# A two-layer attention kernel: other PSUM tiles and an earlier split for the first attention, and another layout for its group norm

## The chip, the cores and the metric

The kernel runs on one core of a Trainium2 chip. The metric is the device time of one launch in microseconds, and the number that counts is the median over repeated runs. Beside the times there is one execution that the hardware profiler recorded; durations of single instructions come from it.

## The reference

The input is 8 images of 32 x 32 positions with 384 channels, all in float32. Two layers are computed, each adding to the residual:

```python
# layer 0
g = group_norm(x)                        # 32 groups of 12 neighbouring channels, over all positions
q, k, v = split(g @ qkv_w + qkv_b)       # 6 heads of 64
s = (q * 64**-0.5) @ k.T + rel_h + rel_w # rel_h[q, kh] = q . table_h[h - kh + 31], rel_w likewise
x = x + softmax(s) @ v @ proj_w + proj_b
# layer 1
t = tokens(x)
a = layer_norm(t)
t = t + softmax(causal((a @ Wq) @ (a @ Wk).T * 384**-0.5)) @ (a @ Wv)   # one head of 384
t = t + ffn(layer_norm(t))   # two linear layers with weights binarised to signs, each output
                             # quantised by the absolute maximum of a group of images; gelu between
```

The quantisation groups are formed over images and only five images get an FFN output; the other three get zero from it.

## The kernel before, in words

The program is written with a tile framework. The author writes the work image by image, and the framework puts the instructions of each engine in an order of its own, with semaphores between engines; each engine then works its queue strictly in that order. Tiles come from pools with a fixed number of buffers: a tile that is asked for when all buffers are taken waits for the oldest to be released. `image` and `page` are SBUF pools with 11 buffers each, `small` has 3. In PSUM there are two score tiles of two banks each (`s_tile`, 128 x 1024) and four tiles of one bank (`o_tile`, 128 x 512).

The stages of one image in layer 0 are these.

- **Group norm** (`group_norm_T`, L299 to L325). The image is loaded channel-major by `load_T` (L293) in three tiles of 128 x 1024. Partition p holds the three neighbouring channels 3p, 3p+1 and 3p+2 (`"(p k) t -> p k t"`), so that a group of 12 is four neighbouring partitions. VectorE takes the statistics of the three channels of a partition together (L306, L307). TensorE sums over the four partitions with the constant matrix `over_group`, once for the mean (L310) and once for the variance (L317). Between these stand small VectorE operations (L312, L314, L315, L318), the square root on ScalarE (L319) and the reciprocal (L320); then the three tiles are normalised (L322). For image b+1 all this runs inside layer 1's attention of image b.
- **Projections** (`queries_keys`, L416). For m = 0 to 5 a 128-column block of the weights gives two heads of q (m = 0 to 2) or k (m = 3 to 5), for the whole image in one two-bank score tile (`project_T`, L361). For each half ScalarE writes the high part (L426, rounded to the matmul's input format) and VectorE the rest (L429). k is also copied with its halves swapped (`ks`, DMAs at L435).
- **Position tables** (`positions`, L443). The products of q with both tables are made in one-bank tiles (L452), copied to a page by ScalarE (L456) and VectorE (L457), and written to DRAM (`far`, L461). DMAs with a shifted stride read the needed diagonals back (`near`, L468).
- **Splits** (`split`, L473). Each 32-row piece of `near` is rounded by ScalarE (L479), the rest is made by VectorE (L480), and both go into `r`, which enters the scores as a third matmul against the constant `unit`. `split(0)` and `split(1)` stand before and after the v projections; `split(2)` is deferred into the attention for every image but the first:

```python
            split(0, near[0])
            for j in range(NJ):
                values(j)
            split(1, near[1])
            later = [lambda: split(2, near[2])]
            if b == 0 or not pools.fast:
                later.pop()()
```

- **v** (`values`, L484): eight projections (L371), copied alternately by ScalarE and VectorE (L485).
- **Attention** (`attend0_fast`): for three pairs of heads p and eight chunks c of keys, scores (L527), exp on ScalarE into a page (L531), running sums on VectorE (L540), and the product with v (L545). The residual with the projection's bias is added on GpSimd (L510).

Layer 1 has its scores at L735, its exp at L743 and its product with v at L749. Its two projection matrices are folded into one by `multiply_out` (wq @ wk.T), which for image 0 loads both matrices and multiplies them just ahead of the first attention. The FFN's last step for image b (`unfinished`) is run inside the projections of image b+1, after m = 3. A second, general path is entered only when the fast path found an overflow; it isn't run here.

Of the kernel before, what the change touches and what calls it, by code (L numbers as in the profile page):

```python
# [27 lines left out]
NP_GN = P // GROUPS_GN  # L28
# [46 lines left out]
def conv_attn_hybrid(  # L75
# [42 lines left out]
    def load_weights(pools):  # L118
# [9 lines left out]
        src = qkv_w.rearrange("(p k) o -> p k o", k=NC)  # L128
# [29 lines left out]
    over_group = const.tile([P, P], F32, name="over_group")  # L158
    nc.gpsimd.memset(over_group, 1.0 / NP_GN)
    for low in (True, False):  # L160

        nc.gpsimd.affine_select(
            out=over_group, in_=over_group, compare_op=ALU.is_ge, fill=0.0, base=0 if low else NP_GN - 1,
            pattern=[[-NP_GN if low else NP_GN, GROUPS_GN], [0, NP_GN]], channel_multiplier=1 if low else -1,
        )
# [104 lines left out]
    def multiply_out(pools):  # L270
# [3 lines left out]
        nc.sync.dma_start(out=wkT_sb, in_=wkT.rearrange("(k p) c -> p k c", p=P))  # L274
        for m in range(NC):
            ps = pools.o_tile(f"wqk_{m}")
            for k in range(NC):
                nc.tensor.matmul(ps[:, :C], wqT_sb[:, k, ts(m, P)], wkT_sb[:, k, :], start=(k == 0), stop=(k == NC - 1))
            nc.vector.tensor_scalar_mul(wqk[:, m, :], ps[:, :C], C**-0.5)

    def stages(pools):
# [9 lines left out]
        def load_T(b):  # L291

            xT = pools.image(f"gnT_{b}")  # L293
            src = img_T[b].rearrange("(p k) t -> p k t", k=NC)
# [4 lines left out]
        def group_norm_T(b, xT=None):  # L299
# [3 lines left out]
            mv = pools.small.tile([P, 2], F32, tag="gmv", name=f"gmv_{b}")  # L303
# [3 lines left out]
            nc.vector.bn_aggr(mv, st.rearrange("p k a s -> p (k a s)"))  # L307

            ps = pools.o_tile(f"gmean_{b}")
            nc.tensor.matmul(ps[:, 0:1], over_group, mv[:, 0:1], start=True, stop=True)  # L310
            cs = pools.small.tile([P, 2], F32, tag="gcs", name=f"gcs_{b}")
            nc.vector.tensor_copy(cs[:, 0:1], ps[:, 0:1])  # L312
            d = pools.small.tile([P, 2], F32, tag="gd", name=f"gd_{b}")
            nc.vector.tensor_tensor(d[:, 0:1], mv[:, 0:1], cs[:, 0:1], ALU.subtract)  # L314
            nc.vector.scalar_tensor_tensor(d[:, 1:2], d[:, 0:1], d[:, 0:1], mv[:, 1:2], ALU.mult, ALU.add)  # L315
            ps = pools.o_tile(f"gvar_{b}")
            nc.tensor.matmul(ps[:, 0:1], over_group, d[:, 1:2], start=True, stop=True)  # L317
            nc.vector.tensor_scalar_add(d[:, 0:1], ps[:, 0:1], 1e-5)  # L318
            nc.scalar.activation(d[:, 0:1], d[:, 0:1], AF.Sqrt)  # L319
            nc.vector.reciprocal(cs[:, 1:2], d[:, 0:1])  # L320
            for k in range(NC):
                nc.vector.tensor_scalar(  # L322
                    xT[:, k, :], xT[:, k, :], cs[:, 0:1], cs[:, 1:2], ALU.subtract, ALU.mult
# [83 lines left out]
        def layer0(b, xT):  # L407
# [8 lines left out]
            def queries_keys(m):  # L416
                p = m % NPAIR
                bias = bqk[:, m : m + 1]
                ps = project_T(wqkv_sb, ts(m, P), xT, f"qk_{b}_{m}")
                dst = [(q if m < NPAIR else k)[par][:, p, :] for par in range(2)]  # L420

                for half in range(2):
                    t = ts(half, T // 2)
                    for par in range(2):
                        hi = rows[par]
                        nc.scalar.activation(dst[par][hi, t], ps[hi, t], AF.Identity, bias=bias[hi])  # L426
                    for par in range(2):
                        hi, lo = rows[par], rows[1 - par]
                        nc.vector.scalar_tensor_tensor(  # L429
                            dst[par][lo, t], ps[hi, t], bias[hi], dst[par][hi, t].bitcast(F32), ALU.add, ALU.subtract  # L430
# [12 lines left out]
            def positions(p):  # L443

                fars = []
                for par in range(2):
                    page = pools.page(f"far_{b}_{p}_{par}")
                    by_col = page.rearrange("i (w h) -> i w h", h=H)
                    for half in range(2):
                        ps = pools.o_tile(f"rel_{b}_{p}_{par}_{half}")  # L450
                        for i in range(2):
# [523 lines left out]
```

## Time and profile before

| what | value |
|---|---|
| median of 8 runs | 2580.23 us (2577.38 to 2581.87) |
| the profiled execution | 2577.29 us, its span 2575.6 us |
| TensorE matmul busy | 2498.8 us, 97% of the span |
| VectorE busy | 1614.4 us, 63% |
| ScalarE busy | 1156.6 us, 45% |
| GpSimd busy | 113.8 us, 4% |
| DMA | 144.70 MB, mean 56 GB/s |
| mean granted TensorE clock | 0.998 of full speed |

The span runs from the first to the last recorded instruction; 1.7 us of the launch lie around it. Busy times of the engines overlap. In the profile PE is TensorE's matmuls, PEld its weight loads, DVE is VectorE, ACT is ScalarE, POOL is GpSimd and SP the queue that issues most DMAs. A float32 matmul of the program is two matmul rows in the profile, one in the rounded format is one. "Idle before, releaser" says how long an engine had nothing to do before an instruction, and what it waited for.

### The profile page before, as it was taken

To read this page: it belongs to the slowest core of one execution; us is meant where nothing else is said; L and a number is where in the kernel's file an instruction comes from. 1 tells how busy PE (TensorE), PEld (TensorE's weight loads), DVE (VectorE), ACT (ScalarE), POOL (GpSimd) and SP (SyncE) were. 2 spreads that over 40 slices of the span, in tenths; PEclk is the share of its full clock that TensorE was granted. 3 is DMA by queue.
4 is the path that set the end of the run, shared out by engine and by line. 5 is a ranking of instruction groups with operands and counts; after the bars stand their busy time and mean duration, and the time that the engine had idled before them with its cause. 6 is when DMAs were issued, how large, how long until landed. Compare 5 with 4: busy or idle time off the path is not lost. (4 is left out here: it accounts for less than half of the span.)

```text
span 2575.6 us, 24797 instructions
## 1 busy us (share of the span) xinstructions
PE 2498.8 (97%) x9378; PEld 1495.0 (58%) x9378; DVE 1614.4 (63%) x2375; ACT 1156.6 (45%) x1513; POOL 113.8 (4%) x103
## 2 busy tenths in 40 slices
PE   7999999999999999999999999999999999999998
PEld 3555685555765556755557555576555555555554
DVE  5895468763587644786546876447764486538652
ACT  4641377421666314764127643156641264127420
POOL 0000002000011000110000100001100010001000
PEclk9999999999999999999999999999999999999999
DMA  6431106011041101150110601003200240015000
GB/s 169 148 147 62 37 1 172 1 62 37 1 123 49 49 13 37 41 131 1 61 37 1 172 1 62 17 21 94 79 25 1 70 103 1 25 42 130 1 1 26
DMA packets 148992, 144.70 MB, mean 56 GB/s; under 512 B 107264, under 2 KB 129664, under 8 KB 147328
## 3 DMA queue, kind: packets, MB, share of 16 engines
q1 hardware_dynamic: 142928, 119.36, 16.5%
q0 software_dynamic: 2880, 23.59, 2.6%
q8 instruction: 76, 1.25, 0.2%
q10 hardware_dynamic: 3056, 0.08, 0.1%
q14 instruction: 52, 0.43, 0.1%
HBM read 75.38 MB, written 42.47 MB: 46 GB/s over the span
## 5 line engine op out<-in xcount | busy, mean ns | idle before, releaser
L531 ACT ACTIVATE f_pr<-f_s 128x1024 f32<-128x1024 f32 x384 | 392.7, 1027 | 401.9 <-PE f_s L527 372.4
L540 DVE TENSOR_TENSOR f_sum<-f_sum,f_pr 128x1024 f32<-128x1024 f32 x288 | 349.0, 1244 | 145.9 <-ACT f_pr L531 144.0
L545 PE MATMUL f_av<-f_pr,f_v 128*64 128x512 f32 x1536 | 359.5, 599 | 0.0
L527 PE MATMUL f_s<-f_q,f_k 128*128 128x512 f32 x768 | 258.2, 417 | 22.5 <-ACT f_pr L531 15.6
L361 PE MATMUL f_qk<-f_gnT,wqkv_sb 128*128 128x512 f32 x576 | 261.7, 599 | 7.3 <-DVE f_k L429 3.3
L527 PE MATMUL f_s<-f_q,f_ks 128*128 128x512 f32 x768 | 244.1, 399 | 0.0
L527 PE MATMUL f_s<-f_r,unit 128*128 128x512 f32 x768 | 241.7, 396 | 0.0
L545 PEld LDWEIGHTS f_av<-f_pr,f_v 128*64 128x64 f32 x1536 | 103.0, 136 | 202.4 <-issue 194.6
L480 DVE TENSOR_TENSOR f_r<-f_near,f_r 32x1024 fp32r<-32x1024 f32 x96 | 193.2, 2012 | 28.7 <-ACT f_r L479 25.9
L527 PEld LDWEIGHTS f_s<-f_q,f_k 128*128 128x128 f32 x768 | 125.0, 189 | 139.2 <-issue 51.9
L735 PE MATMUL f_s<-f_q,f_lnT 128*128 128x512 f32 (+3 forms) x576 | 197.2, 488 | 0.0
L749 PE MATMUL f_av<-f_v,f_pr 128*128 128x385 f32 x576 | 194.5, 486 | 0.0
L361 PEld LDWEIGHTS f_qk<-f_gnT,wqkv_sb 128*128 128x128 f32 x576 | 108.0, 191 | 123.5 <-issue 110.0
L527 PEld LDWEIGHTS f_s<-f_q,f_ks 128*128 128x128 f32 x768 | 145.2, 189 | 35.8
L527 PEld LDWEIGHTS f_s<-f_r,unit 128*128 128x128 f32 x768 | 144.9, 189 | 34.4
L749 PEld LDWEIGHTS f_av<-f_v,f_pr 128*128 128x128 f32 x576 | 108.6, 190 | 78.6 <-issue 11.5
L479 ACT CAST f_r<-f_near 32x1024 fp32r<-32x1024 f32 x96 | 145.9, 1520 | 2.4
L735 PEld LDWEIGHTS f_s<-f_q,f_lnT 128*128 128x128 f32 x576 | 101.4, 190 | 73.9 <-issue 50.2
L371 PE MATMUL f_v<-wqkv_sb,f_gnT 128*128 128x384 f32 x384 | 129.4, 490 | 10.5 <-ACT f_v L485 8.3
L850 DVE TENSOR_REDUCE am<-f_h 128x1 f32<-128x1024 f32 (+2 forms) x80 | 71.6, 946 | 96.6 <-ACT f_h L843 96.6
L843 ACT ACTIVATE f_h<-f_y,b_sb 128x256 f32<-128x256 f32 x240 | 100.8, 472 | 67.0 <-PE f_y L839 67.0
L743 ACT ACTIVATE f_pr<-f_s 128x1024 f32<-128x1024 f32 (+3 forms) x64 | 41.7, 651 | 194.4 <-DVE f_s L740 194.4
(153 smaller groups left out, 3325.4 us busy)
## 6 DMA issues: line engine op xcount, KB each, us to landing
f_far<-f_far SPq DMA_DIRECT2D x48, 512.0 KB, 3.0
f_ks<-f_k SPq DMA_DIRECT2D x96, 256.0 KB, 5.1
f_gnT<-in_xT SPq DMA_DIRECT2D x24, 512.0 KB, 4.6
f_near<-f_far SPq DMA_DIRECT2D x96, 128.0 KB, 3.8
f_x<-in_x SPq DMA_DIRECT2D x32, 384.0 KB, 6.7
out_y<-f_x SPq DMA_DIRECT2D x32, 384.0 KB, 4.0
f_w1a<-w1s POOLq DMA_DIRECT2D x5, 1536.0 KB, 7.2
f_w2a<-w2s POOLq DMA_DIRECT2D x5, 1536.0 KB, 6.7
```

The costliest lines, as they stand in the source:

```text
L361: nc.tensor.matmul(ps[:, half, :], w[:, k, cols], xT[:, k, ts(half, 512)], start=(k == 0), stop=(k == NC - 1),)
L371: nc.tensor.matmul(ps[:, :C], xT[:, k, ts(j, P)], w[:, k, cols], start=(k == 0), stop=(k == NC - 1))
L479: nc.scalar.copy(dst[ts(hi, 32)], src)
L480: nc.vector.tensor_tensor(dst[ts(lo, 32)], src, dst[ts(hi, 32)].bitcast(F32), ALU.subtract)
L527: nc.tensor.matmul(sc[:, half, :], keys[:, ts(c, P)], queries[:, ts(half, 512)], start=(i == 0), stop=(i == 2))
L531: nc.scalar.activation(pr, sc.rearrange("p a n -> p (a n)"), AF.Exp)
L540: nc.vector.tensor_tensor(sums[par], prev, prs[par], ALU.add)
L545: nc.tensor.matmul(avs[half][ts(par, HD), :], v[:, c, ts(h, HD)], prs[par][:, ts(half, 512)], start=(c == 0), stop=(c == NJ - 1),)
L735: nc.tensor.matmul(sc[:, half, lo:], xT[:, c // 4, k, ts(c % 4, P)], q[:, half, k, lo:], start=(k == 0), stop=(k == NC - 1),)
L749: nc.tensor.matmul(av[:, : C + 1], prs[c][:, ts(j - c, P)], v[:, c, :], start=(c == 0), stop=(c == j))
L843: nc.scalar.activation(pairs[i][:, m, :, :], ps[:, ts(i % 2, 256)].rearrange("p (j q) -> p j q", j=2), AF.Identity, bias=b1_sb[:, m : m + 1],)
L850: nc.vector.tensor_reduce(am[:, i, n - 1 : n], pairs[i][:, cuts[n - 1] : cuts[n], :, :], AX.XYZ, ALU.max, apply_absolute_value=True)
```

## The change

Six things are changed together.

1. Group norm: the channels are laid out in the usual way, channel 128 k + p on partition p (`"(k p) t -> p k t"`, for the weights too). A group of 12 lies across partitions of one tile or of two. Statistics are taken per channel, and each step over groups is three small matmuls: to 32 groups with `to_group` (L326), and back to the channels with `of_group` (L334), for the mean and again for mean and scale. So there are four steps instead of two.
2. k (and q of image 0) is projected into a one-bank tile per half (L457). q of the other images stays in score tiles.
3. The table products of p = 1 and 2 (and of all p for image 0) go into score tiles, with one copy of 64 x 1024 on each engine (L499, L500).
4. The splits of p = 1 and 2 are made for both heads at once (`split_both`, L521 and L522) into the pages that held the tables, and eight DMAs per pair bring the rows to `r` (L526). All are written ahead of the attention; nothing is deferred.
5. After `unfinished`, a one-element exp with scale 0 is run on ScalarE.
6. wq.T and wk.T are loaded at the start (`load_qk`, L282), and `multiply_out` stands among the first image's projections.

```diff
         def load_T(b):
             xT = pools.image(f"gnT_{b}")
-            src = img_T[b].rearrange("(p k) t -> p k t", k=NC)
+            src = img_T[b].rearrange("(k p) t -> p k t", p=P)
...
-            nc.vector.bn_aggr(mv, st.rearrange("p k a s -> p (k a s)"))
-            ps = pools.o_tile(f"gmean_{b}")
-            nc.tensor.matmul(ps[:, 0:1], over_group, mv[:, 0:1], start=True, stop=True)
-            cs = pools.small.tile([P, 2], F32, tag="gcs", name=f"gcs_{b}")
-            nc.vector.tensor_copy(cs[:, 0:1], ps[:, 0:1])
-            d = pools.small.tile([P, 2], F32, tag="gd", name=f"gd_{b}")
-            nc.vector.tensor_tensor(d[:, 0:1], mv[:, 0:1], cs[:, 0:1], ALU.subtract)
-            nc.vector.scalar_tensor_tensor(d[:, 1:2], d[:, 0:1], d[:, 0:1], mv[:, 1:2], ALU.mult, ALU.add)
-            ps = pools.o_tile(f"gvar_{b}")
-            nc.tensor.matmul(ps[:, 0:1], over_group, d[:, 1:2], start=True, stop=True)
-            nc.vector.tensor_scalar_add(d[:, 0:1], ps[:, 0:1], 1e-5)
-            nc.scalar.activation(d[:, 0:1], d[:, 0:1], AF.Sqrt)
-            nc.vector.reciprocal(cs[:, 1:2], d[:, 0:1])
+                nc.vector.bn_aggr(mv[:, k, :], st[:, k, :, :].rearrange("p a s -> p (a s)"))
+            def over_groups(src, name):
+                ps = pools.o_tile(name)
+                for k in range(NC):
+                    nc.tensor.matmul(
+                        ps[:GROUPS_GN, 0:1], to_group[:, k, :], src(k), start=(k == 0), stop=(k == NC - 1)
+                    )
+                return ps[:GROUPS_GN, 0:1]
+            def to_channels(src, n, name):
+                ps = pools.o_tile(name)
+                for k in range(NC):
+                    nc.tensor.matmul(ps[:, k * n : (k + 1) * n], of_group[:, ts(k, P)], src, start=True, stop=True)
+                return ps[:, : NC * n].rearrange("p (k n) -> p k n", k=NC)
+            gm = pools.small.tile([GROUPS_GN, 2], F32, tag="gm", name=f"gm_{b}")
+            nc.vector.tensor_copy(gm[:, 0:1], over_groups(lambda k: mv[:, k, 0:1], "gmean"))
+            mc = to_channels(gm[:, 0:1], 1, "cmean")
+            d = pools.small.tile([P, NC, 1], F32, tag="gd", name=f"gd_{b}")
+            nc.vector.tensor_tensor(d, mv[:, :, 0:1], mc, ALU.subtract)
+            nc.vector.tensor_tensor(d, d, d, ALU.mult)
+            nc.vector.tensor_tensor(d, d, mv[:, :, 1:2], ALU.add)
+            var = pools.small.tile([GROUPS_GN, 1], F32, tag="gvar", name=f"gvar_{b}")
+            nc.vector.tensor_scalar_add(var, over_groups(lambda k: d[:, k, :], "gvar"), 1e-5)
+            nc.scalar.activation(var, var, AF.Sqrt)
+            nc.vector.reciprocal(gm[:, 1:2], var)
+            cs = pools.small.tile([P, NC, 2], F32, tag="gcs", name=f"gcs_{b}")
+            nc.vector.tensor_copy(cs, to_channels(gm, 2, "cstat"))
...
             def queries_keys(m):
-                ps = project_T(wqkv_sb, ts(m, P), xT, f"qk_{b}_{m}")
+                both = project_T(wqkv_sb, ts(m, P), xT, f"qk_{b}_{m}") if b and m < NPAIR else None
                 for half in range(2):
                     t = ts(half, T // 2)
+                    if both is None:
+                        ps = pools.o_tile(f"qk_{b}_{m}_{half}")
+                        for i in range(NC):
+                            nc.tensor.matmul(
+                                ps, wqkv_sb[:, i, ts(m, P)], xT[:, i, t], start=(i == 0), stop=(i == NC - 1)
+                            )
+                    else:
+                        ps = both[:, t]
...
             def positions(p):
-                    for half in range(2):
-                        ps = pools.o_tile(f"rel_{b}_{p}_{par}_{half}")
...
+                    n = 1 + (p > 0 or b == 0)
+                    for part in range(2 // n):
+                        ps = pools.s_tile(f"rel_{b}_{p}_{par}") if n == 2 else pools.o_tile(f"rel_{b}_{p}_{par}_{part}")[:, None, :]
...
+                        nc.scalar.copy(page[:HD, ts(part, n * 512)], ps[:HD])
                         nc.vector.tensor_copy(
+                            by_col[HD:, :, ts(part, n * H // 2)], ps[HD:].rearrange("i (h w) -> i w h", w=W)
                         )
...
+            def split_both(p, near, pages):
+                for d in range(2):
+                    hi, lo, src = (t[ts(d, HD)].rearrange("k (h w) -> k h w", h=H) for t in (*pages, near))
+                    if d:
+                        src = near[ts(d, HD)].rearrange("k (w h) -> k h w", h=H)
+                    nc.scalar.copy(hi, src)
+                    nc.vector.tensor_tensor(lo, src, hi.bitcast(F32), ALU.subtract)
+                for i in range(2):
+                    for d in range(2):
+                        for par in range(2):
+                            nc.sync.dma_start(
+                                out=r[par][ts(2 * i + d, 32), p, :].bitcast(F32),
+                                in_=pages[i][ts(2 * d + par, 32)].bitcast(F32),
+                            )
...
+                if m == NPAIR + 1 and sides_qk:
+                    multiply_out(pools, *sides_qk.pop())
                 if m == NPAIR and unfinished:
                     unfinished.pop()()
+                    early = pools.small.tile([P, 1], F32, tag="early", name=f"early0_{b}")
+                    nc.scalar.activation(early, k[1][:, 0, T - 1 :].bitcast(F32), AF.Exp, scale=0.0)
+                if m == NPAIR + 1:
+                    split(0, near[0][0])
-            split(0, near[0])
             for j in range(NJ):
                 values(j)
-            split(1, near[1])
-            later = [lambda: split(2, near[2])]
-            if b == 0 or not pools.fast:
-                later.pop()()
+            split_both(1, *near[1])
+            split_both(2, *near[2])
             if pools.fast and b == 0:
                 join_biases(pools)
-                multiply_out(pools)
...
         def run(pools):
             gn = load_T(0)
             if pools.fast:
                 load_weights(pools)
+                sides_qk.append(load_qk(pools))
```

## The prediction, made before the changed kernel was run

> **What bounds the kernel now.** I read the page first, then TensorE's waits, then busy time over the eight stretches that the change rebuilds, then the timelines of ACT, PE and DVE where a wait ends.
>
> The page (engine, busy us, share, instructions; then the granted clock by slice):
>
> ```profile
> span 2575.6 us, 24797 instructions
> ...
> PE 2498.8 (97%) x9378; PEld 1495.0 (58%) x9378; DVE 1614.4 (63%) x2375; ACT 1156.6 (45%) x1513; POOL 113.8 (4%) x103
> ...
> L479 ACT CAST f_r<-f_near 32x1024 fp32r<-32x1024 f32 x96 | 145.9, 1520 | 2.4
> ```
>
> TensorE is the bound: 2575.6 - 2498.8 = 76.8 us idle. A change can win only from those holes, or from TensorE's own work. Its waits (who waited for whom: us, times, longest):
>
> ```profile
> PE f_s L527 <- ACT f_pr L531: 15.6, 15, 1.9
> PE f_gmean L310 <- DVE gmv L307: 11.3, 1, 11.3
> PE f_v L371 <- ACT f_v L485: 8.3, 8, 1.1
> ...
> PE f_s L527 <- DVE f_k L429: 4.1, 5, 0.8
> ...
> PE f_qk L361 <- DVE f_k L429: 3.3, 5, 1.0
> ...
> PE f_s L527 <- ACT f_far L456: 2.8, 3, 0.9
> PE f_v L371 <- DVE f_far L457: 2.2, 5, 0.5
> ```
>
> Seven kinds, nearly all where an image goes from projections into attention. That stage by image 0, 1, 2, 5, 6, 7 (length; PE, PEld, DVE, ACT, POOL busy; clock):
>
> ```profile
> 50.00:92.00 42.00, 36.38 (x120) 21.75 (x118) 33.29 (x32) 36.66 (x37) 0.00 (x0) 1.00 0.74 187
> 388.00:446.00 58.00, 52.87 (x165) 28.23 (x163) 49.17 (x59) 44.04 (x51) 12.66 (x10) 1.00 0.74 190
> 733.00:791.00 58.00, 52.95 (x165) 28.28 (x164) 49.05 (x59) 44.06 (x51) 12.76 (x10) 1.00 0.73 190
> ...
> 1769.00:1827.00 58.00, 53.48 (x165) 29.71 (x165) 47.65 (x58) 43.05 (x51) 12.86 (x10) 0.97 0.71 190
> 2040.00:2098.00 58.00, 55.27 (x169) 29.41 (x168) 45.61 (x46) 44.30 (x53) 6.77 (x1) 1.00 0.66 163
> 2309.00:2367.00 58.00, 55.20 (x170) 29.38 (x169) 45.51 (x46) 44.48 (x53) 7.56 (x1) 1.00 0.66 163
> ```
>
> PE idle is length less busy: 5.62, 5.13, 5.05, 4.52, 2.73, 2.80; images 3 and 4 have 5.32 and 5.11, together 36.3 us. The worst hole, on ACT in image 5:
>
> ```profile
> 1813.25 0.48 ACT L485 COPY f_v<-f_v 128x384 f32<-128x384 f32 x1
> 1813.75 1.28 ACT L531 ACT_TABLE_LOAD   x1
> 1815.04 1.94 ACT L531 ACTIVATE f_pr<-f_s 128x1024 f32<-128x1024 f32 x2
> ```
>
> TensorE, out of score tiles, resumes at 1816.12 after 1.87 us; the table load is most of it. The group norm as it now runs inside layer 1's attention:
>
> ```profile
> 1982.13 0.28 PE L310 MATMUL f_gmean<-gmv,over_group 128*128 128x1 f32 x2
> 1982.27 1.96 PE L735 MATMUL f_s<-f_q,f_lnT 128*128 128x512 f32 x4
> 1984.07 0.28 PE L317 MATMUL f_gvar<-gd,over_group 128*128 128x1 f32 x2
> 1984.21 1.96 PE L735 MATMUL f_s<-f_q,f_lnT 128*128 128x512 f32 x4
> ```
>
> Score rows start right behind it: no stop.
>
> **What one stop costs.** Idle is not all. Paired score rows on an undisturbed path start 0.46 us apart (780.37 to 780.83), the first pair after the stop at 779.80 takes 0.57: 0.11 more. And a row shown as 0.39 long has its successor 0.23 later, so 0.16 of each hole is drawn as busy. A stop costs its idle plus 0.27.
>
> **The parts.**
>
> *k in one-bank tiles, table products in two-bank tiles, splits ahead.* ACT's second half of k no longer waits behind VectorE's 0.75 us L429 on the same tile; the far copies are one 64x1024 on each engine instead of two of 64x512; the splits of p 1 and 2 become 2 + 2 instructions per pair instead of 4 + 4. By L479's 1.52 us mean, four ACT casts fewer per image are 6.1 us, and about as much on VectorE. Both run beside TensorE (ACT 44 of 58 us busy, VectorE 49), so this counts only through the holes. Image 2, walked in the changed program's order with before's durations: 0.521 and 0.827 (k), 0.441 (far) and 0.336 vanish. The v wait of 1.03 shrinks to 0.5: ACT still runs casts ahead of the v copy. New: about 0.9 at a two-bank product that waits for qk_2's score tile, and 0.2 at v_3.
>
> *exp's table early* (images 1 to 5; in 6 and 7 the sqrt and exp loads are elsewhere, and their hole here is 0.4). The 1.28 us load and one tiny activation move to ACT's slack beside the k projections (14 of 58 us), and the 1.9 us hole goes; next late is the v copy. If ACT were late there, 1.28 would come back at k. The Trainium skill, "ScalarE: Activation LUTs", section "What ACT_TABLE_LOAD costs", puts each switch at about 2.66 us, 1.28 of load and 1.38 of drain. The row shows no drain: copy ends 1813.73, load 1813.75 to 1815.03, exp 1815.04. By the page the five holes would shrink by 5 x 1.38 = 6.9 us more than I count.
>
> *What comes in.* The split rows are now written into the far pages and carried to r by 16 more 128 KB DMAs per image on SP. Near's DMAs of that size land in 3.8 us; p=1's rows are wanted some 40 us later. They stand behind the ks DMAs on SP, but ahead of f_x, whose add on POOL (L510, 7.2 us, up to 8.0) starts later; f_x has slack. The pages stay taken longer, and VectorE's last split subtraction stands ahead of the first sums (L540, 1.24 us each), which free pages for exp. I expect a wait of 1.0 us in image 1 to 5 (0 if the sums keep up, 2 if not; middle taken). The order also divides one more av pair per image there: a lone pair holds the queue 1.01 us (2089.32 to 2090.33) instead of 0.43; I take 0.4, as part replaces one that exists now.
>
> Images 1 to 5: idle 25.13 / 5 = 5.03, plus 6 stops x 0.27 = 6.65 now. After: 0.9 + 0.2 + 0.5 + 3 x 0.27 = 2.41, page wait 1.27, pair 0.4: 4.08. Gain 2.6 each, 13.0 in all (bounds: nothing to 5 each).
> Images 6, 7: 2.77 + 4 x 0.27 + 0.6 (a divided pair, gone) = 4.45 now; after 0.5 + 0.4 + 2 x 0.27 = 1.44. Gain 3.0 each, 6.0.
>
> *Clock.* In 1816.3 to 1819.7 the granted clock was 0.51, right behind the 1.87 us hole, and likewise behind the 1.82 us hole at 1470.5: 3.4 us at half pace, 1.7 lost, twice. Without those holes, 3.4 gained (0 if another hole triggers it). The Trainium skill, "TensorE: Matmul & The Clock Gate", section "What's actually happening", lets the clock fall only after about 3.4 us of idleness; holes of 1.8 would be harmless and this term would be 0. The rows have the drop, so I keep 3.4.
>
> *Image 0.* Idle 5.62 + 5 x 0.27 = 6.97. The wq @ wk.T matmuls (18 rows, about 0.32 us each by 384-column v rows) fill among the projections, but the exp load stays; I take half, 3.5 (0 to 6). Against it the longer start: gmean to gvar took 11.29 to 12.54 with two cold loads of 0.25 per step; four steps of six, less the sqrt load's present wait, make 3.3 (2 to 4.5). The wqT and wkT loads (1.18 MB) now stand on SP among the start's loads: at the 169 GB/s of the page's first slice 7 us of transfer, over before the first table product's DMA (first far copy at 30.3); no cost taken, up to 2 in the bounds. Together +0.2.
>
> *Group norm, images 1 to 7.* 24 tiny rows instead of 4, in four steps, with TensorE's order putting one score matmul pair (0.86) between steps. A load of 128 columns costs 0.11 (two gmean rows push the scores by 0.22). Twelve such: 1.3. Twelve of 32 columns, not in the trace, cost between 0.03 and 0.11 each by width and by that row: middle 0.8. Less today's 0.45: 1.65. Hops: matmul to VectorE 0.29, 0.15 to 0.22 per operation, three operations at the longest: about 0.9 against 0.94 cover. A v copy (0.56) may stand ahead on VectorE, as at 1982.34; 0.25 for that. 1.9 each (1.2 to 3.5): 13.3 lost.
>
> **Sum.** 13.0 + 6.0 + 3.4 + 0.2 - 13.3 = 9.3 us. The profiled execution took 2577.29 (span 2575.6 plus 1.7 around it), 2.94 below the median 2580.23. 2577.3 - 9.3 = 2568.0, and on the median 2571. About 0.2% (5.2 us) is what a measurement here can tell from no change.
>
> **Rivals.**
> 1. *Pages (slower).* The sums fall under POOL's 7.2 us add (VectorE's L480 took 8.52 at worst where 1.2 is usual), pages run out and exp of p=0 stops, so score tiles do. For: less room on 11 pages, far ones held. Against: VectorE has 16% slack and PE's waits on exp are short. Beyond 2.3 us per image (9.3 / 8 more than I count, plus my 1.0) the gain is gone; at 4 extra x 8 = 32, about 2603. Chance 0.14.
> 2. *Hops stop TensorE (slower).* If the three further hops are not covered, each costs up to what 11.29 to 12.54 shows, 1.25: 7 x 3 x 1.25 = 26 more, 2597; at half, 2584. For: cover is equal to the hop by 0.04. Chance 0.14.
> 3. *The holes only move.* ACT still does casts ahead of v and VectorE is no shorter: images 1 to 5 gain 1.5 instead of 2.6, images 6 and 7 1.5 instead of 3.0: 8.5 less, 2579.5. For: L480's 1.9 us median on VectorE is as long in the new form, and v still waits for ACT. Against: the table load alone is 1.28 of each 1.9 us hole. Chance 0.16.
> 4. *All holes go.* 5 x 5 + 2 x 4 + 3.4 + 1 - 10 = 27: 2553. For: ACT and VectorE have 14 and 9 us free per stage. Against: the walk finds four new or left waits. Chance 0.14.
> My forecast: 0.42.
>
> Range 2554 to 2590: it leaves out rival 1's upper part and the little below rival 4. Faster (below 2575) 0.60: rival 4, 0.39 of the forecast's 0.42, 0.07 of rival 3. Same 0.14: 0.03 of the forecast, 0.07 of rival 3, 0.04 of rival 2. Slower (above 2585.4) 0.26: rival 1, 0.10 of rival 2, 0.02 of rival 3.
>
> **What would show it.** Right: PE idle in the stage of images 1 to 5 near 3 us, no hole of 1.8 us on exp, no clock of 0.5 mid-run, tiny matmul steps 0.5 to 0.9 us apart from the scores with little idle, first projection of image 0 about 3 us later. Wrong: waits of PE on f_pr in p=0 above 2 us, behind L540's successor; idle behind the group means' matmuls; r's DMAs landing late.

## The result

The changed kernel takes 2586.25 us (median of 11 runs, 2578.49 to 2588.14) against 2579.76 for the kernel before (31 runs): the ratio is 1.0023, with a 95% interval of 1.0015 to 1.003. It is 6 us slower, where 9 us less had been forecast. Its profiled execution took 2580.74 us, 5.5 less than the median; the run with GpSimd's add moved (below) shows what that difference may be.

The page of the changed kernel, the same two lines as before:

```profile
span 2579.0 us, 25377 instructions
...
PE 2521.3 (98%) x9538; PEld 1509.4 (59%) x9538; DVE 1554.5 (60%) x2341; ACT 1104.2 (43%) x1452; POOL 106.0 (4%) x106
```

TensorE's idle time fell from 76.8 to 57.7 us, as the change meant it to, but its busy time rose by 22.5: partly the group norm's rows, partly rows that ran at half clock. Its waits:

```profile
PE f_s L587 <- ACT f_pr L591: 9.0, 17, 1.1
...
PE f_den L647 <- DVE f_sum L600: 5.0, 1, 5.0
PE f_den L635 <- ACT f_oT L624: 4.5, 1, 4.5
...
PE f_v L401 <- ACT f_v L543: 0.5, 3, 0.2
```

The waits on k and on the table copies are gone, the one on v fell from 8.3 to 0.5. Two single waits of 5.0 and 4.5 us are new. The next view shows the stage between projections and attention in images 2, 5 and 6, then the two stretches at half clock (start and end; length; PE, PEld, DVE, ACT, POOL busy; clock):

```profile
744.90:802.90 58.00, 57.68 (x191) 32.71 (x190) 46.28 (x56) 40.28 (x47) 5.46 (x9) 1.00 0.83 207
1781.00:1839.00 58.00, 57.65 (x192) 32.08 (x192) 46.02 (x55) 40.52 (x46) 5.46 (x9) 1.00 0.89 221
2048.00:2106.00 58.00, 57.80 (x187) 31.54 (x185) 39.48 (x42) 39.23 (x46) 0.00 (x0) 1.00 0.73 170
148.80:155.60 6.80, 5.02 (x15) 3.96 (x16) 6.01 (x20) 3.95 (x5) 0.48 (x1) 0.50 0.01 3
206.80:213.70 6.90, 5.42 (x9) 1.77 (x10) 3.85 (x5) 0.00 (x0) 5.24 (x1) 0.51 0.37 151
```

Idle in the stage is 0.2 to 0.4 us, where 4.5 to 5.1 (images 2 and 5) and 2.7 (image 6) stood before. So the stage did better than forecast, and the time went elsewhere. Distances between the starts of matching score rows in the two traces say where. When image 0's layer 1 begins, the changed kernel is 10.1 us behind; each of seven group norms adds 2.41 us, 16.9 in all; each first attention of images 1 to 7 wins back 2.8 to 4.0, 24 in all. 10.1 + 16.9 - 24 = 3, the difference of the spans (3.4).

Image 0 is the surprise. The two new stops, on ACT, on TensorE and on VectorE:

```profile
148.95 1.07 ACT L624 COPY f_oT<-f_av 128x512 f32<-128x512 f32 x2 [11.27 <-DVE sums_w L240]
```

```profile
149.59 0.43 PE L635 MATMUL f_den<-few,fold 128*64 128x32 f32 x4 [4.53 <-ACT f_oT L624]
151.00 1.22 PE L587 MATMUL f_s<-f_q,f_k 128*128 128x512 f32 x2 [0.99 <-ACT f_pr L591]
```

```profile
134.69 7.36 DVE L240 TENSOR_REDUCE sums_w<-f_w 128x1 f32<-128x614 f32 x15
141.97 3.48 DVE L600 TENSOR_TENSOR f_sum<-f_sum,f_pr 128x1024 f32<-128x1024 f32 x3
145.37 3.55 DVE L240 TENSOR_REDUCE sums_w<-f_w 128x1 f32<-128x608 f32 x5
```

In image 0 VectorE also takes the sums and signs of the FFN weights. The attention output f_oT needs a buffer of the pool in which those raw weights lie, and gets it when the reductions L240 have read them. They run at 134.7 to 148.9, 37 us later than before, when they began at 97.6 and ended at 116.8. Two of their rows in the kernel before:

```profile
97.60 1.48 DVE L228 TENSOR_REDUCE sums_w<-f_w 128x1 f32<-128x614 f32 x2
...
113.20 3.55 DVE L228 TENSOR_REDUCE sums_w<-f_w 128x1 f32<-128x608 f32 x5
```

In the changed kernel ACT stands at the copy for 11.3 us, with the exps behind it, and TensorE stops; the signs come late as well, and the sums of p = 2 behind them.

### The profile page after: what moved, and what is told of

It is laid out like the page before. It is cut to its first block, busy times and chain, and to the rows that moved or that the text cites. A ratio compares the mean times of both kernels' runs of the same rounds, so it can differ in the third digit from the quotient of the medians.

```text
span 2579.0 us, 25377 instructions
## 1 busy us (share of the span) xinstructions
PE 2521.3 (98%) x9538; PEld 1509.4 (59%) x9538; DVE 1554.5 (60%) x2341; ACT 1104.2 (43%) x1452; POOL 106.0 (4%) x106
## 3 DMA queue, kind: packets, MB, share of 16 engines
q8 instruction: 78, 1.28, 0.2%
## 4 chain that ended last, share of the span: by engine, by line
PE 88%; ACT 5%; DVE 4%; issue 1%; DMA 1%; ACTq 0%; POOL 0%; POOLq 0%; DVEq 0%
PE f_s L587 20%; PE f_av L605 12%; PE f_v L401 8%; PE f_s L793 7%; PE f_av L807 7%; PE f_y L897 6%; PE f_qk L457 5%; PE f_q L755 5%; PE f_y L936 4%; PE f_qk L391 4%; PE f_pj L401 2%; PE f_rel L494 2%; PE f_pj L690 2%; ACT f_r L537 1%; PE f_pt L303 1%
## 5 line engine op out<-in xcount | busy, mean ns | idle before, releaser
L600 DVE TENSOR_TENSOR f_sum<-f_sum,f_pr 128x1024 f32<-128x1024 f32 x288 | 379.5, 1351 | 150.2 <-ACT f_pr L591 149.0
L807 PEld LDWEIGHTS f_av<-f_v,f_pr 128*128 128x128 f32 x576 | 108.6, 190 | 78.6 <-issue 11.5
L457 PE MATMUL f_qk<-f_gnT,wqkv_sb 128*128 128x512 f32 x324 | 147.3, 602 | 1.2 <-DVE f_gnT L352 1.2
L755 PE MATMUL f_q<-f_lnT,wqk 128*128 128x512 f32 x288 | 127.5, 592 | 0.0
L401 PE MATMUL f_v<-wv_sb,f_lnT 128*128 128x384 f32 x384 | 126.5, 486 | 0.0
```

Source lines behind the costliest of these rows:

```text
L401: nc.tensor.matmul(ps[:, :C], xT[:, k, ts(j, P)], w[:, k, cols], start=(k == 0), stop=(k == NC - 1))
L457: nc.tensor.matmul(ps, wqkv_sb[:, i, ts(m, P)], xT[:, i, t], start=(i == 0), stop=(i == NC - 1))
L600: nc.vector.tensor_tensor(sums[par], prev, prs[par], ALU.add)
L755: nc.tensor.matmul(ps, wqk[:, k, ts(m, P)], xT[:, half, k, :], start=(k == 0), stop=(k == NC - 1))
L807: nc.tensor.matmul(av[:, : C + 1], prs[c][:, ts(j - c, P)], v[:, c, :], start=(c == 0), stop=(c == j))
```

## The experiments

All times are medians, and every kernel was timed beside the kernel before, which took 2580.85 to 2583.44 us in these comparisons. The changed kernel itself was timed only in the first comparison, at 2586.25. "Less" and "more" are against that, unless another kernel is named; such differences are good to some 3 us, and smaller ones say nothing.

**The loads on another queue.** My first theory was SP's queue: the raw weights' first load is issued at 95.8 us (74.1 before), behind the 16 split DMAs.

```diff
-                    nc.sync.dma_start(out=w, in_=...)
+                    (nc.gpsimd if name == "w" else nc.sync).dma_start(out=w, in_=...)
```

> The changed kernel, with one edit: the loads of the raw FFN weights that feed the sums over groups are issued by GpSimd instead of SP, so that they no longer stand behind the 16 new split DMAs of image 0. Queue theory: these loads start at 74 us or earlier (95.8 in the changed kernel), VectorE's reductions over them run before 120 us again (134.7 to 149 now), the attention output of image 0 gets its buffer in time, and TensorE's stops of 4.5 + 1.0 us near 150 us and 5.1 us near 208 us go, with the half clock behind both: 13 to 17 us less, 2570 to 2573. Rival, pages: the sums of image 0 are late because the split holds VectorE and the pages; then the queue of the weight loads matters little, and the time stays within 4 us of 2586.

2577.45 (0.9981, 0.9972 to 0.999): 9 less, not 13 to 17. The reductions run at 79 to 101 now, but a stop of 6.2 us on exp stands at 102.6, since the sums that free pages wait behind reductions, and one of 2.3 at 214.7. The stops moved; the queue was not all of it.

**The old split in image 0 alone.**

```diff
-                        at = 2 * d + par if p else 2 * par + d
+                        at = 2 * d + par if p and b else 2 * par + d
...
-            split_both(1, *near[1])
-            split_both(2, *near[2])
+            for p in (1, 2):
+                split_both(p, *near[p]) if b else split(p, near[p][0])
```

> The changed kernel, but image 0 splits p = 1 and 2 the old way, in 32-row pieces straight into r, so it issues no split DMAs; images 1 to 7 are as in the changed kernel. Queue theory: as in the run with the other queue, 10 to 17 us less (2569 to 2576), with the weight loads on SP right behind the ks DMAs near 75 us. Theory that the early products of wq and wk and the buffer of their weights, and not the queue, make the attention output of image 0 wait: the stops remain, and the time is within 4 us of 2586.

2577.16 (0.9981, 0.9973 to 0.999), again 9 less. The first loads are issued at 70.9 to 81.5, earlier than in the kernel before up to the second one, yet the reductions start at 110.5, not 97.6: they stand behind ten sums in VectorE's queue. Stops of 3.2 and 3.8 us are left. So early loads do not make early reductions.

**The old group norm,** code as in the front part.

> The changed kernel with the group norm of the kernel before (three neighbouring channels on a partition, two steps of one matmul), everything else as changed. From the distances of the score rows in the two traces the new group norm costs 2.4 us on TensorE for each of seven images and 1.2 us at the start: 18 us less, 2568. Rival: part of that time covers waits that would come back elsewhere (exp or sums), and only half is won, about 2577. The stops of image 0 stay in either case.

2567.74 (0.9942, 0.9927 to 0.9957): 18.5 less. Six executions lie between 2562 and 2570, so the median alone is good to some 4 us; seven times 2.41 and 1.2 at the start, by distances of score rows in the traces, make 18.1. The stops of image 0 stay (4.5, 1.0 and 5.1 us). The norm's cost is its own.

**Both edits.**

> Both of the last two edits at once: the old group norm, and the old split in image 0. If the two costs are independent, their gains add: 18 + 10 to 17, so 2551 to 2558, some 25 us faster than the kernel before. If the stops of image 0 hang on the exact times at its start, the sum is missed by more than 4 us.

2558.83 (0.9906, 0.9892 to 0.992): 27.4 less, against 18.5 + 9.1 = 27.6. They add.

**The new group norm in the kernel before.**

> The kernel before with the new group norm alone. If the norm's cost is its own (weight loads and refilled score rows on TensorE, no waits that the other parts hide), it is the mirror image of the run with the old norm: 18 us slower than the kernel before, a ratio of 1.007. Rival: in the kernel before other waits swallow part of it, and it is 10 us or less, 1.004.

2601.12 (1.0077, 1.0061 to 1.0093): the mirror image, 18.5 more than the 2582.59 beside it. TensorE's order shows where 2.41 us per image go:

```profile
1987.83 0.35 PE L326 MATMUL f_gmean<-gmv,to_group 128*32 128x1 f32 x6
1988.11 1.12 PE L793 MATMUL f_s<-f_q,f_lnT 128*128 128x512 f32 x2
1989.17 0.82 PE L334 MATMUL f_cmean<-gm,of_group 32*128 32x1 f32 x6
1989.92 1.12 PE L793 MATMUL f_s<-f_q,f_lnT 128*128 128x512 f32 x2
1990.98 0.35 PE L326 MATMUL f_gvar<-gd,to_group 128*32 128x1 f32 x6
1991.26 1.12 PE L793 MATMUL f_s<-f_q,f_lnT 128*128 128x512 f32 x2
1992.31 0.83 PE L334 MATMUL f_cstat<-gm,of_group 32*128 32x2 f32 x6
```

(These rows are of the changed kernel, image 5's layer 1.) From one start to the next, the steps take 0.28, 0.75, 0.28 and 0.76: 2.07. The score pairs between them take about 1.06 instead of 0.86: another 0.2 for each of four returns to the rows of 512 columns (refills), 0.8. 2.87 less the old norm's 0.45 is 2.42. There is no stop in it: one score pair covers each hop.

**Without the early exp.** (The three lines of part 5 are left out.)

> The changed kernel without the one-element exp, so that exp's table is loaded at the first score tile again in images 1 to 5. Theory: the stop of 1.3 to 1.9 us on the first exp tiles comes back five times with 0.27 us of refill, and now and then the half clock behind it (1.7 us): 8 to 16 us slower than the changed kernel, 2594 to 2602. Rival: with the splits ahead of it ACT has slack there, the load is hidden by the projections of v, and the time stays within 3 us of 2586.

2582.5 (1.0001, 0.9992 to 1.0011): 4 less instead of 8 to 16 more. From the first score tile to the end of chunk 2 images 1 to 5 take 7.2 us with or without it; p = 1 takes 39.4 without and 40.3 with. So the stop on the table load did not come back, and the 0.9 of p = 1 makes up the 4 us; the run with the old split (below) shows what may lie behind it. In this kernel the early exp is worth nothing.

**k of images 1 to 7 in score tiles.**

```diff
-                both = project_T(...) if b and m < NPAIR else None
+                both = project_T(...) if b else None
```

> The changed kernel with k of images 1 to 7 projected into two-bank score tiles, as before. Theory: the k stops of the kernel before (0.5 and 0.8 us in images 1 to 5, 0.9 in 6 and 7) come back, with refill 7 x 1.2 to 1.8: 8 to 13 us slower, 2594 to 2599. Rival: the stop came from ACT's far copies and not from the tile; then it is within 3 us of 2586.

2683.66 (1.039, 1.037 to 1.041): 97 more, ten times the forecast. With q, k, table products and scores all in two score tiles, TensorE waits on nearly every turn:

```profile
PE f_s L587 <- DVE f_r L538: 22.5, 7, 3.2
PE f_rel L494 <- DVE f_k L467: 18.5, 7, 3.3
...
PE f_qk L391 <- DVE f_far L500: 9.7, 5, 2.6
```

and the half clock comes back twice in each of images 1 to 5.

**The table products in one-bank tiles.**

```diff
-                    n = 1 + (p > 0 or b == 0)
+                    n = 1
```

> The changed kernel with all table products in one-bank tiles, two copies of 512 columns on each engine, as before. Theory: the far stops of the kernel before return (0.44 us in images 1 to 5, about 0.9 in 6 and 7, each with 0.27 of refill) and VectorE and ACT get about 1 us more work per pair: 5 to 8 us slower than the changed kernel, 2591 to 2594. Rival: k's one-bank tiles had already removed these stops, and it stays within 3 us of 2586.

2636.81 (1.0207, 1.0185 to 1.0229): 51 more, not 5 to 8. Now k, tables and v share four one-bank tiles (f_qk waits 26.0 us for table copies on VectorE). Parts 2 and 3 are one exchange of tiles between two users; with one half taken away it is worse by more than the whole is worth (some 35 us, below).

**The old split in all images,** `split` as in the kernel before, the third deferred.

> The changed kernel with the old split in all images: 32-row pieces straight into r, no split DMAs, the third pair deferred into the attention again. Image 0 is then as in the run with its old split (9 us less than the changed kernel). Theory: in images 1 to 7 the split ahead is worth the stop on v (1.0 us) and the short one on exp (0.35), each with its refill, against the wait at the start of p = 1 (1.1 us) and the lone pair of the product with v: within 0 to 1.5 us per image, so 2577 to 2588. Rival: the new split is the main gain of the stage, 3 us per image: 2598.

2565.39 (0.9932, 0.9918 to 0.9947): 21 less, outside both theories. The new split is a loss also after image 0. One piece is not put back: the change also moved `split(0)` one projection earlier, ahead of m = 5, and here it stays there. By distances of score rows in images 1 to 5, old to new split: to the end of chunk 2 from 9.0 to 7.2 (1.8 won), rest of p = 0 from 25.2 to 26.5, p = 1 from 37.5 to 40.3 (1.2 and 2.8 lost). Part of the 2.8 can be seen in TensorE's order at the start of p = 1 (changed kernel, image 2):

```profile
822.58 0.73 PE L587 MATMUL f_s<-f_q,f_k 128*128 128x512 f32 x2
823.15 0.62 PE L587 MATMUL f_s<-f_q,f_ks 128*128 128x512 f32 x2
823.60 0.63 PE L587 MATMUL f_s<-f_q,f_k 128*128 128x512 f32 x2
824.07 0.63 PE L587 MATMUL f_s<-f_q,f_ks 128*128 128x512 f32 x2
824.53 0.62 PE L587 MATMUL f_s<-f_r,unit 128*128 128x512 f32 x2
826.26 0.49 PE L587 MATMUL f_s<-f_q,f_k 128*128 128x512 f32 x1 [1.11 <-ACT f_pr L591]
```

Both score tiles are opened before the rows with r, which close a tile, have been put in for the first. So neither tile can go to exp until the second row with r has ended, at 825.15 (the exp starts at 825.19), and the third score block has no tile to go to. With the old split each tile gets its six rows in one piece there, and the wait is absent. In the run without the early exp the first of these r rows comes one row earlier, and the wait is 0.42 instead of 1.11. That the planner put the r rows late because r now comes by DMA is plausible, but not shown.

**Less for VectorE in image 0.**

```diff
-            for g in range(NG):
-                nc.vector.tensor_reduce(part[:, times[which], which, g : g + 1], ..., AX.XY, ALU.add)
+            nc.vector.tensor_copy(part[:, times[which], which, :], w[:, 0, :NG])
```

> The run with the old split in image 0, and without the 20 reductions over the FFN weights (VectorE, 11 us in image 0's attention): the means are replaced by a few copied numbers, so the sums over the weights are left out and the signs are other ones. Theory that VectorE is full in image 0 (92 percent busy from 62 to 205 us in the kernel before): with 11 us less the stops of 3.2 and 3.8 us near 137 and 207 shrink or go, with the half clock behind them: 6 to 11 us less than that run's 2577, so 2566 to 2571. Rival, order alone: the stops hang on what stands in front of what on VectorE; one of them stays, and it is 0 to 4 us less.

2567.32 (0.994, 0.9922 to 0.9958): 10 less than the run with the old split in image 0; no stop of image 0 is left after 17 us, and no half clock while TensorE works. My theory was that VectorE is full in image 0. A window over its attention shows the kernel before, the changed one, and the changed one with late products (the last run below):

```profile
62.00:205.00 143.00, 137.48 (x556) 76.82 (x556) 131.86 (x177) 73.21 (x70) 8.24 (x4) 1.00 0.47 155
62.00:205.00 143.00, 135.00 (x543) 76.97 (x541) 112.95 (x162) 68.76 (x68) 1.11 (x2) 0.98 0.44 140
62.00:205.00 143.00, 138.15 (x558) 77.08 (x557) 124.14 (x170) 63.13 (x63) 8.89 (x4) 1.00 0.54 172
```

DVE has 131.86 of 143 us in the kernel before (92%), 112.95 in the changed one (79%) and 124.14 with late products. Of these three the one with the stops has VectorE least busy, and the last, with all its reductions, has none of them. So the place of the work in VectorE's order makes the stops, and a full VectorE does not explain them. This run cannot tell the two apart: leaving work out shortens the queue in either reading.

**GpSimd's add later.**

```diff
-                        if p == 0 and b > 0:
+                        if p == 1 and b > 0:
                             xt = residual()
```

> The changed kernel with GpSimd's add of the bias to the residual moved from p = 0 to p = 1 in images 1 to 7. Theory: in the changed kernel this add (807.8 to 814.6 in image 2) stands over the last sums of p = 0 on VectorE, six of which take 11.9 us instead of 7, so that the sums are set aside late and exp waits at the start of p = 1 (1.1 us idle); moved, that wait goes in images 1 to 5 and p = 1 takes 1.3 to 2.5 us less each: 6 to 12 us less, 2574 to 2580. Rival: the wait comes from the pages that the split holds; it stays, within 3 us of 2586.

2580.32 (0.999, 0.9981 to 1.0): 6 less, the lower end of the theory's range, but not as it said. The wait of 1.11 us at the start of p = 1 stays in images 1 to 5; p = 1 falls from 40.3 to 39.1 by something else in it. The theory of that wait is wrong, and the order shown above is the reading that remains. This trace shows another thing, at the end of image 0's attention: the last six sums take 13.35 us under GpSimd's add.

```profile
203.56 13.35 DVE L600 TENSOR_TENSOR f_sum<-f_sum,f_pr 128x1024 f32<-128x1024 f32 x6
```

```profile
208.55 7.28 POOL L570 TENSOR_TENSOR f_x<-f_x,pb 128x3072 f32<-128x3072 f32 x1 [9.39 <-DMA f_gnT<-in_xT]
```

In the profiled execution of the changed kernel they were through at 209.4:

```profile
202.47 6.89 DVE L600 TENSOR_TENSOR f_sum<-f_sum,f_pr 128x1024 f32<-128x1024 f32 x6
```

```profile
208.46 7.43 POOL L570 TENSOR_TENSOR f_x<-f_x,pb 128x3072 f32<-128x3072 f32 x1 [10.40 <-DMA f_gnT<-in_xT]
```

By its single rows it is one addition that waits: it starts at 209.24, after GpSimd's add, lasts 7.68 us and ends 1.09 after the add; the others take 1.22, and so does one that began just before the add. In the changed kernel both late sums had begun before the add and were not stretched. The stretch from the end of p = 2 to layer 1 is 38.8 us here against 32.6 there. The trace without the early exp is like this one (13.35, and 39.2). In both the stop near 206 us is longer, and the half clock behind it lasts 13.65 us instead of 6.83. That 6 us is the size by which the median of the changed kernel lies above its profiled run: 11 of its 13 executions took 2585 to 2588 us, the profiled one and one other 2581 and 2578. That the two groups differ by the place of that one addition fits, but only one execution was profiled, so it is not shown.

**A first version from the parts that pay.** It keeps the tiles, the early exp and the early products, with the old norm and split, and moves the last signs behind image 0's attention.

> A version put together from the runs: k and table tiles, the early products and the early exp of the changed kernel, the group norm and the split of the kernel before, and the last third of the FFN weights' signs moved out of image 0's attention, behind it. If the gains add, the old split everywhere (2565) less 18.5 for the norm is 2547, and 2539 to 2543 if VectorE's relief in p = 2 of image 0 takes away the stop near 205 us with its half clock. Rival: the moved signs delay the projection or layer 1 of image 0 instead, and it is 2547 or above.

2544.19 (0.9849, 0.9826 to 0.9873): the sum of the gains and little from the moved signs. The stop at 205 us goes, but one of 3.6 us appears where the projection waits for the residual; 3.2 us at 135.5 stays.

**The early exp with the old split.**

> The changed kernel with the old split in all images (2565) and without the one-element exp. Theory: with the old split ACT is held by casts ahead of the first exp, as in the kernel before, so the table load of 1.28 us shows there: the stretch to the end of chunk 2 (9.0 us with the early exp) grows by 1.3 to 1.9 us in images 1 to 5, 6 to 10 us in all, 2571 to 2575, and the half clock may follow. Rival: the better tiles alone give ACT the slack, as in the run with the new split; within 2 us of 2565.

2571.7 (0.9961, 0.9946 to 0.9975): 6.3 more than with it, 1.26 for each of five images; the two traces show 1.1 each (10.1 instead of 9.0 us to the end of chunk 2). With the old split ACT has casts ahead of the first exp, and the table load counts in full; with the new one it was hidden by the v projections anyway. The Trainium skill, "ScalarE: Activation LUTs", section "What ACT_TABLE_LOAD costs", adds 1.38 us of drain to the 1.28 of the load. By these two figures five loads would make an estimated 13 us; the 6.3 measured shows no drain on the path.

**The products back in their old place, old split.**

```diff
-                if m == NPAIR + 1 and sides_qk:
-                    multiply_out(pools, *sides_qk.pop())
...
                 join_biases(pools)
+                multiply_out(pools, *load_qk(pools))
```

> The changed kernel with the old split in all images (2565) and with wq.T and wk.T loaded and multiplied just ahead of image 0's attention again. Theory: the products only fill stops in image 0, whose attention is bounded by VectorE anyway; within 3 us of 2565. Rival: they are filler that the projections of image 0 need, 4 to 6 us slower; or the other way, the buffer of their weights frees the loads of the FFN weights later, and moving them back gains 3 us or more.

2556.67 (0.9905, 0.9891 to 0.9919): 8.7 less. The reductions are back at 95.3 to 114.5, and image 0 has no new stop and no half clock.

**Three parts only:** that kernel with the old norm, so only parts 2, 3 and 5 are left of the change, and the earlier place of `split(0)`.

> Only the tiles of k and of the tables and the early exp of the changed kernel; group norm, split and the place of wq @ wk.T as in the kernel before. If all gains add: 2557 for the run with the old split and late products, less 18.5 for the old norm, 2538; some 41 us or 1.6 percent below the kernel before. Rival: the start or the first attention of image 0 gives part of it back, 2543 or more, no better than the version put together before (2544).

2538.49 (0.982, 0.98 to 0.984), as summed. It beats both kernels, the one before by 1.8%.

**The changed kernel with the products in their old place.**

> The changed kernel with wq.T and wk.T loaded and multiplied just ahead of image 0's attention again, all else as changed, the split DMAs of image 0 too. Theory that both the split DMAs and the early products move VectorE's reductions over the FFN weights behind the sums: either alone leaves stops of about 8 us with the half clock, so 2577 or so, 9 us less than the changed kernel. Rival, SP's queue decides alone: the stops stay, within 3 us of 2586. Rival, the products decide alone: 2568 to 2571.

2571.38 (0.9948, 0.9929 to 0.9967): 15 less, nearly what the theory of the products alone said. The 16 split DMAs stand on SP as in the changed kernel, the first raw weights are issued at 88.7, later than in either run with 2577, and yet:

```profile
97.38 0.56 DVE L294 TENSOR_SCALAR wqk<-f_wqk 128x384 f32<-128x384 f32 x1 [1.38 <-PE f_wqk L293]
97.86 2.18 DVE L240 TENSOR_REDUCE sums_w<-f_w 128x1 f32<-128x614 f32 x3
...
100.42 1.48 DVE L240 TENSOR_REDUCE sums_w<-f_w 128x1 f32<-128x614 f32 x2
102.23 1.23 DVE L599 TENSOR_TENSOR f_sum<-f_sum,f_pr 128x1024 f32<-128x1024 f32 x1 [0.33 <-ACT f_pr L590]
```

The reductions run between the sums again, at 97.9 to 115.3. The scores of image 0's layer 1 begin at 226.0 us in this kernel, at 237.7 in the changed one and at 227.5 in the kernel before. With that my first theory falls: the loads' place on SP matters less than where the products stand. In the old place, as I read it, the products give TensorE work inside the attention and VectorE time for the reductions; in the new one TensorE is ahead, VectorE has holes while it waits for exp (109 to 133), and then everything at once. Why the planner sets the reductions behind the sums in the one case is not shown.

## Why the prediction was wrong

The runs make a ladder from the kernel before to the changed one. Its steps compare medians of different comparisons, so each is good to some 3 us:

| step | median us | step by medians | span us | step by spans |
|---|---|---|---|---|
| kernel before | 2579.8 | | 2575.6 | |
| parts 2, 3, 5: tiles, early exp; `split(0)` earlier | 2538.5 | -41.3 | 2535.0 | -40.6 |
| + part 1, group norm | 2556.7 | +18.2 | 2555.1 | +20.1 |
| + part 4, new split | 2571.4 | +14.7 | 2566.6 | +11.5 |
| + part 6, early products | 2586.3 | +14.9 | 2579.0 | +12.4 |

Two of the steps depend on their order: the early products cost 14.9 us with the new split and 8.7 with the old one, the new split 14.7 with late products and 20.9 with early ones. What the place of `split(0)` is worth alone no run shows; it is part of the 41.3.

Against the terms of the sum:

- **Image 0, "+0.2": the step that failed.** The products were to "fill among the projections", their loads had "no cost taken, up to 2 in the bounds", half of the stage's holes were counted as won. They were won: the scores of p = 1 begin 3.8 us earlier than before. Then 13.9 us were lost, so that layer 1 begins 10.1 late: p = 1 takes 8.0 us longer than before, the stretch from the end of p = 2 to layer 1 6.4. I costed the moved step by its own rows and by SP's queue, and not by what it does to VectorE's fixed order in the attention behind it: the weight reductions moved behind sums that come late, ACT waited 11.3 us for the buffer that they free, and TensorE stopped. Putting the products back alone takes 15 us away, with the stops. That the other steps of the ladder make 2571.4, where 2571 was forecast, is luck: the tiles and the early exp won 41 us where 22.4 were counted (13.0, 6.0 and 3.4), and the new split took 15 back.
- **Holes in images 1 to 7: right in sum, wrong inside.** 2.6 and 3.0 us were forecast per image, 2.8 to 4.0 came. But the stage was worth twice that (all holes went, and the feared waits of 0.9, 0.2 and 0.5 did not come), and the new split took the surplus. The kernel of three parts shows what the tiles and the early exp were worth by themselves, with `split(0)` earlier: 41 us.
- **New split: wrong sign.** It was counted among the gains, with a page wait of 1.0 against it. The wait came (1.11 us), but from the order of the score rows and at p = 1; the rest of p = 0 lost 1.2 and p = 1 2.8, where 1.0 and 0.4 had been counted. In all 12 to 15 us lost with the products late, 21 with them early.
- **Early exp: right size, wrong company.** 1.28 us per image is about what it is worth with the old split (1.1 by the traces, 1.26 by medians). With the new split it is worth nothing.
- **Clock: right and then undone.** The half-clock stretches of images 4 and 5 are gone; image 0 has two of 6.8 us instead. The Trainium skill, "TensorE: Matmul & The Clock Gate", section "What's actually happening", asks for some 3.4 us of idleness in a free-running window. The stops of 4.5 and 5.1 us fit that: the half clock began inside them, 3.7 and 3.6 us after their start. The holes of 1.82 and 1.87 us in images 4 and 5 of the kernel before, which also brought the half clock, do not. Holes of that size in images 1 to 3 brought none, and their place in time tells them apart. In each of the two traces the drops of the clock stand on a grid of 3.413 us, and half clock lasts one or two steps of it: 1471.60 and 1816.35 in the kernel before are 101 such steps apart, 148.81 and 206.83 in the changed one 17. The holes of images 4 and 5 lie whole between two marks of that grid; a mark cuts each of the other three, leaving at most 1.67 us on one side. So a free-running window fits, but here 1.82 us of idleness in one was enough.
- **Group norm: 16.6 forecast (13.3 and 3.3 at the start), 18.2 to 18.5 measured.** The weight loads were near (0.28 and 0.75 per step; I had 0.4 and 0.65), hops (the way from TensorE to VectorE and back between the steps) cost nothing, and the refill of four score pairs (0.8 us) was not in the sum. The start cost 1.2 instead of 3.3, as the sums of the first two tiles run while the third is still loading.
- **Rivals.** The first, sums under GpSimd's add, happens: it stretches one sum at the end of image 0 in two runs, and one under the add at the end of p = 0 in images 1 to 7 of the changed kernel (in image 2 one takes 6.26 us). But it is not what stops exp there: with the add moved, the wait of 1.11 us stayed. The second, uncovered hops, did not happen, and neither did the third, that the holes only move: 0.2 to 0.4 us are left in the stage. The fourth, all holes gone, is what parts 2, 3 and 5 do alone, and more than it said.

## What to carry to other kernels

When a step is moved, look at the stage that it leaves, and at the order of the other engines' work there. Here TensorE's lead of 3.8 us became a delay of 10.1, because VectorE's order put the reductions that free a buffer behind sums that come late. The busy share did not tell: VectorE stood at 79% with the stops and at 87% without them. Parts that trade the same tiles must be costed as one: the whole exchange of k and tables gained some 35 us (41.3 less the early exp's 6.3, the earlier `split(0)` included), and taking away one half of it cost 97 or 51.

## What the chip showed that I had not expected

Six one-column matmuls with weight loads of 32 columns take 0.28 us and six with loads of 128 columns 0.75, the change to the next rows included, but every return to the big rows costs 0.2. One VectorE addition of 1.22 us that started under a GpSimd add of 7.3 us lasted 7.68 and ended 1.09 after it, so that six sums took 13.35 us instead of 6.89; one that had begun before the add was not stretched. Half clock began inside the stops of 4.5 and 5.1 us and lasted 6.8 us each time; 1.8 and 1.5 of these were idle, so that some 2.5 and 2.7 us were lost by the slower rows besides the stops.
